# The first pair's rows picked by matmuls of zeros and ones, the first four pairs cut by half of the queries, and one more drain on GpSimd

## The chip, the core and the metric

One core of a Trainium2 chip runs the whole program. The core has five engines, each with a queue of its own that it works off in order: TensorE (PE, with its weight loads shown as PEld), VectorE (DVE), ScalarE (ACT), GpSimd (POOL) and SyncE (SP, which here only issues transfers). Transfers are issued from the queues of SP, ACT and POOL and are carried out by 16 DMA engines. The metric is the device time of one execution in microseconds (us), less being better.

## The reference

Four batches of 1,024 rows of 256 numbers go through an attention layer with 16 heads of 16 numbers, a layer norm, a mixture of eight experts of which each row takes two, and a second layer norm. The change lies in the attention; its core, cut to what matters:

```python
q = einsum('bsc,oc->bso', x, wq)            # k and v likewise, then split in 16 heads of D = 16
q_mag, k_mag = softplus(q), softplus(k)
q_embed = stack([q_mag * cos(qp), q_mag * sin(qp)])   # 32 numbers for each head and row
k_embed = stack([k_mag * cos(kp), k_mag * sin(kp)])   # kp is qp and a bias of the head
attn = softmax(einsum('bhsd,bhtd->bhst', q_embed, k_embed) / sqrt(D))
x = layernorm(x + (attn @ v) @ wo)
x = layernorm(x + experts(x))               # top 2 of 8, each with room for 640 rows
```

## The kernel before

**Work.** A batch has 16 heads, taken as 8 pairs, four in each of two groups f of 8 heads. A pair's scores are 2 heads x 1,024 queries x 1,024 keys. They are made twice. First, row by row of queries (`score_half`, L684, the matmul on L693), only to take the maxima: each 128x512 block is reduced on VectorE (L697). Then, with keys on the partitions, in `key_scores` (matmul L725), the maxima are subtracted by a small matmul of ones with two rows (L740), ScalarE takes the exponential (L747), and TensorE multiplies with the values (L761). Before that second pass, `max_parts` (L699 on) splits the 2 heads x 2 halves of maxima into two numbers each and `max_rows` transposes them (L716) and copies them (L718).

**Steps.** The loop on L971 walks 256 steps: a pair has eight, one for each 128 keys. A step holds four matmuls of each of the kinds L693 (for the next pair's maxima), L725 and L740, two exponentials of 128x1024 and eight matmuls of L761, plus what the table `todo` hangs on it: embeddings of later heads, transposes of x, values, stores.

**Embeddings.** `embedding` (L353) makes 8 heads' worth of q or k for 512 rows: a matmul (L370), softplus on ScalarE (L387 to L389), its last sum on VectorE or GpSimd (L391 or L393), the product with a table of cos and sin (L399), and a split in a rounded part and a rest (L404/L406 and L408), since the score matmuls read tiles of the type `F32R`. It leaves them with (position in the head, head) on the partitions. A pair needs another order: 32 numbers of one head below each other, parts repeated. The kernel gets this by storing the embedding in DRAM (L416) and loading the rows that a pair wants (`load_qk`, L421, transfers on L435 and L439), for every pair, the first too.

**The start.** Before the loop (L902 to L963) x is transposed (L322), the four embeddings of group 0 (k and q, two halves of 512 rows each) are made in their fast form (all of it on ScalarE and VectorE), stored and loaded again; q's on GpSimd's queue, k's on SP's. Then come all 32 maxima of pair 0 with, beside them, the values (L339) and one embedding of group 1, both halves of its q; `second_key_table` makes group 1's table of angles on ScalarE and GpSimd. Only then `max_parts(0)`, `max_rows(0)` and step 0. Step 0 also holds eight score matmuls of pair 1.

**The order** is written by hand (`tc.manual_schedule`): each engine takes its instructions in the order of the program text.

**The end.** Each expert's output rows are sent by indirect transfers from GpSimd's queue (`sent`, L1193; L1170 and L1269 are the others). The last expert sends five blocks as they come from VectorE. The program ends on L1346, where every engine drains and they meet.

Of the kernel before, what the change touches and what calls it, by code (L numbers as in the profile page):

```python
# [28 lines left out]
def kernel(  # L29
# [72 lines left out]
    with ExitStack() as actx:  # L102
# [70 lines left out]

        w_in = {w: aconst.tile([P, KC, DIM], F32, name=f"w{w}_sb") for w in "qk"}
# [39 lines left out]
        def key_table(h):  # L214

            cols = halves[h]
            for i, c in enumerate((nb4, sb4)):
                nc.vector.tensor_scalar(kt0[:, i, cols], cs[:, 1 - i, cols], c[:, 0:1], None, ALU.mult)
            for i in range(2):
                nc.vector.scalar_tensor_tensor(  # L220
                    kt0[:, i, cols], cs[:, i, cols], cb4[:, 0:1], kt0[:, i, cols],
                    ALU.mult, ALU.add,
                )

        def second_key_table(h):

            cols = halves[h]
            a = p4.tile([P, 2, HS], F32, tag="pt", name=f"kta_{h}")
            kt = p4.tile([P, 2, HS], F32, tag="pt", name=f"kt_{h}")
            for i, c in enumerate((nb4, sb4)):  # L230
                nc.scalar.activation(a[:, i, :], cs[:, 1 - i, cols], AF.Copy, scale=c[:, 1:2])
                nc.scalar.activation(kt[:, i, :], cs[:, i, cols], AF.Copy, scale=cb4[:, 1:2])
            for i in range(2):
                nc.gpsimd.tensor_tensor(kt[:, i, :], kt[:, i, :], a[:, i, :], ALU.add)
            store_table(2, h, kt)
# [117 lines left out]
        def embedding(b, f, w, h, fast=False, tab=None, pauses=()):  # L353
# [14 lines left out]
            ps = bank(f"ep_{name}", fast)  # L368
# [32 lines left out]
            parts = p2.tile([P, 2, 2, HS], F32R, tag="parts", name=f"parts_{name}")  # L401
            for i in range(2):
                if fast:
                    nc.scalar.copy(parts[:, 0, i, :], e[:, i, :])  # L404
                else:
                    nc.gpsimd.tensor_copy(parts[:, 0, i, :], e[:, i, :])  # L406
            for i in range(2):
                fine.tensor_tensor(  # L408
                    parts[:, 1, i, :], e[:, i, :], parts[:, 0, i, :], ALU.subtract
                )  # L410
            yield
            to = embed[b, f, w]
            by = nc.gpsimd if fast and w == "q" else nc.sync
            for p in range(2):
                for i in range(2):
                    by.dma_start(  # L416
                        to[2 * p + i, :, :, cols].rearrange("d m s -> (d m) s"),
                        parts.bitcast(F32)[:, p, i, :],
                    )

        def load_qk(u, cols=slice(0, S), what="qk", by=nc.sync):  # L421


            b, p = divmod(u, NU)
            f, p = divmod(p, NU // NF)
            if u not in qks:
                qks[u] = big.tile([P, 4, S], F32R, tag="big", name=f"qk_{u}")
            raw = qks[u].bitcast(F32)
            for h in range(2):
                q, k = (  # L430
                    embed[b, f, w][:, :, 2 * p + h, cols].rearrange("k d s -> (k d) s") for w in "qk"
                )
                for i in range(4 if "q" in what else 0):
                    lo = 32 * (i // 2)
                    by.dma_start(  # L435
                        raw[32 * i : 32 * (i + 1), 2 * h, cols], q[lo : lo + 32, :]
                    )
                for i in range(2 if "k" in what else 0):
                    by.dma_start(raw[64 * i : 64 * (i + 1), 2 * h + 1, cols], k)  # L439
# [244 lines left out]
        def score_half(u, k, j):  # L684


            i, s = divmod(k, 4)
            if u not in nms:
                nms[u] = small.tile([P, 4, 4, 2], F32, tag="nm", name=f"nm_{u}")
            qk, h = qks[u], s % 2  # L690
            lo = HS * (s // 2) + P * i
            ps = bank(f"s_{u}_{k}_{j}")
# [4 lines left out]
            nc.vector.tensor_reduce(nms[u][:, i, s, j : j + 1], ps, AX.X, ALU.max, negate=True)  # L697

        def max_parts(u):  # L699

            nm = nms.pop(u)
            m = m_sb[u % 2].rearrange("p i (s c) -> p i s c", c=32)
            both = small.tile([P, 4, 4, 2], F32, tag="nm_parts", name=f"nm_parts_{u}")
            nc.vector.tensor_reduce(both[:, :, :, 0], nm, AX.X, ALU.min)
# [7 lines left out]
        def max_rows(u, rotate=False):  # L712

            ps = bank(f"mp_{u}", rotate)
            for i in range(4):
                nc.tensor.transpose(ps[:, i * P : (i + 1) * P], m_sb[u % 2][:, i, :], ident)  # L716
            mts[u] = p2.tile([P, 512], F32R, tag="mt", name=f"mt_{u}")
            nc.scalar.copy(mts[u], ps)  # L718

        def key_scores(u, c, h):  # L720

            qk = qks[u]
            ps = ps_st.tile([P, 2, HS], F32, tag="st", name=f"st_{u}_{c}_{h}")
            for f in range(2):
                nc.tensor.matmul(  # L725
                    ps[:, f, :],
                    qk[:, 2 * h + 1, c * P : (c + 1) * P],
                    qk[:, 2 * h, f * HS : (f + 1) * HS],
# [5 lines left out]
        def exponentials(u, c, tiles):  # L734

            for f in range(2):
                for h in range(2):
                    s = 2 * f + h
                    rows = slice(32 * s, 32 * s + 2)
                    nc.tensor.matmul(  # L740
                        tiles[h][:, f, :], ones_r[rows, :], mts[u][rows, :],
                        start=False, stop=True,
                    )
            pts[u, c] = []
            for h in range(2):
                pt = p4.tile([P, 2, HS], F32, tag="pt", name=f"pt_{u}_{c}_{h}")
                nc.scalar.activation(pt, tiles[h], AF.Exp)  # L747
                pts[u, c].append(pt)

        def weighted_values(u, c):  # L750

            if c == 0:
                avs[u] = ps_1.tile([P, 512], F32, tag="av", name=f"av_{u}")
            av, pt = avs[u], pts.pop((u, c))
            p = u % NU
            f, p = divmod(p, NU // NF)
            for n in range(2):
                cols = slice(n * DIM, (n + 1) * DIM)
                for s in range(4):
                    h = s % 2  # L760
                    nc.tensor.matmul(  # L761
                        av[32 * s : 32 * (s + 1), cols],
                        va[f][:, c, 2 * p + h, :],
                        pt[h][:, s // 2, cols],
                        start=(c == 0 and n == 0),
                        stop=(c == NT - 1 and n == 1),
                    )
            if c == NT - 1:
                av_sb = p2.tile([P, 512], F32, tag="avs", name=f"avs_{u}")
                nc.scalar.copy(av_sb, av)  # L770
                avs[u] = av_sb
                if by_rows(u):
                    collect(u)

        def by_rows(u):
            return u < B * NU - NU // NF

        def collect(u):

            b, p = divmod(u, NU)  # L780
            f, p = divmod(p, NU // NF)
            if p == 0:
                nums[b, f] = p2.tile([P, 2, HS], F32, tag="num", name=f"num_{b}_{f}")
                sums[b, f] = dram.tile([2, FH, HS], F32, name=f"sums_{b}_{f}")
            av_sb = avs.pop(u)
            for n in range(2):
                for h in range(2):
# [562 lines left out]
```

## Time and profile before

| what | us |
|---|---|
| time, median of 3 runs (1432.48 to 1434.82) | 1434.66 |
| the profiled execution | 1435.0 |
| its span, first to last instruction | 1433.2 |
| TensorE busy | 1360.3 (95%) |
| VectorE busy | 888.3 (62%) |
| ScalarE busy | 732.8 (51%) |
| GpSimd busy | 410.5 (29%) |
| maxima on VectorE, L697, 1,024 of 684 ns | 646.3 |
| exponentials, L747, 512 of 1021 ns | 496.2 |

The page cuts the span in 40 slices of 35.8 us and gives each engine's busy share in each as a digit in tenths; PEclk is the share of its full clock that TensorE was granted. The answers of the trace by stretches of time give the same in microseconds, with the count of instructions in brackets; the timeline lists instructions by start and duration, equal neighbours merged, with the idle time before them and what ended it. TensorE's ends are modelled, so that neighbouring durations overlap; start to start is the surer reading.

### The profile page before, as it was taken

What the parts mean: (1) busy time and instruction counts of PE and PEld (TensorE: products, weight loads), DVE (VectorE), ACT (ScalarE), POOL (GpSimd) and SP (SyncE); (2) the same over time, 40 slices, a digit from 0 to 9 for tenths busy, and PEclk for the clock granted to TensorE, in tenths of its full rate; (3) what the DMA queues carried; (4) which work ended last, traced back from release to release, by engine and by line L of the source; (5) the groups of instructions that cost most, each with busy time, mean ns of one, the idle gap of its engine ahead of it and who ended that gap; (6) DMA issues with size and microseconds to landing.
All of it is one profiled execution on the core that took longest, in us unless ns stands there. A gap on an engine that the chain in (4) does not pass through costs nothing. (4 is left out here: it accounts for less than half of the span.)

```text
span 1433.2 us, 24396 instructions
## 1 busy us (share of the span) xinstructions
PE 1360.3 (95%) x9314; PEld 856.8 (60%) x9314; DVE 888.3 (62%) x1930; ACT 732.8 (51%) x1000; POOL 410.5 (29%) x436
## 2 busy tenths in 40 slices
PE   5899999999999999999999999999995499999996
PEld 3455555656655565565556556555643277777775
DVE  7767766667876666787766567787724343333334
ACT  5365666565556656556675755655562122222221
POOL 5640034250001647100065530000301314444542
PEclk8899999999999999999999999999997699999998
DMA  7856367374543746454466452234210445334211
GB/s 241 257 177 189 101 170 207 87 233 107 151 122 95 225 145 181 116 165 99 129 183 190 126 169 65 64 84 118 74 64 3 138 152 183 110 122 133 77 44 40
DMA packets 107315, 191.23 MB, mean 133 GB/s; under 512 B 19633, under 2 KB 56178, under 8 KB 107072
## 3 DMA queue, kind: packets, MB, share of 16 engines
q1 hardware_dynamic: 96192, 167.80, 40.4%
q0 software_dynamic: 9888, 20.01, 4.5%
q10 hardware_dynamic: 1120, 1.87, 0.4%
q8 instruction: 73, 1.20, 0.4%
q14 instruction: 42, 0.34, 0.1%
HBM read 119.32 MB, written 73.63 MB: 135 GB/s over the span
## 5 line engine op out<-in xcount | busy, mean ns | idle before, releaser
L697 DVE TENSOR_REDUCE nm<-s 128x1 f32<-128x512 f32 x1024 | 646.3, 684 | 240.5 <-PE s L693 232.2
L747 ACT ACTIVATE pt<-st 128x1024 f32<-128x1024 f32 x512 | 496.2, 1021 | 371.1 <-PE st L740 360.3
L693 PE MATMUL s<-qk 128*128 128x512 f32 x1024 | 387.9, 438 | 13.6 <-DVE parts_q L408 8.3
L725 PE MATMUL st<-qk 128*128 128x512 f32 x1024 | 307.1, 399 | 3.2 <-ACT pt L747 3.1
L761 PE MATMUL av<-pt,va 128*32 128x256 f32 x4096 | 274.7, 385 | 0.5 <-ACT pt L747 0.5
L693 PEld LDWEIGHTS s<-qk 128*128 128x128 f32 x1024 | 179.6, 190 | 121.4 <-DVE nm L697 49.9
L725 PEld LDWEIGHTS st<-qk 128*128 128x128 f32 x1024 | 181.9, 188 | 66.4 <-ACT pt L747 33.1
L761 PEld LDWEIGHTS av<-pt,va 128*32 128x32 f32 x4096 | 107.0, 109 | 107.2 <-issue 61.8
L644 POOL DMA_INDIRECT slots_in<-held,scatter_idx x64 | 62.7, 979 | 290.0 <-DVE scatter_idx L640 211.9
L393 POOL TENSOR_TENSOR soft_q<-y_q,soft_q 128x512 f32<-128x512 f32 x14 | 17.9, 1280 | 441.6 <-ACT soft_q L389 441.6
L1251 PE MATMUL op<-w,h 128*128 128x256 f32 x640 | 144.1, 379 | 0.0
L1232 PE MATMUL hp<-slots_t,w 128*128 128x320 f32 x512 | 140.4, 435 | 0.0
L740 PE MATMUL st<-mt,ones_r 2*128 2x512 f32 x1024 | 129.3, 494 | 0.7 <-ACT mt L718 0.7
L1251 PEld LDWEIGHTS op<-w,h 128*128 128x128 f32 x640 | 119.4, 190 | 15.9
L1232 PEld LDWEIGHTS hp<-slots_t,w 128*128 128x128 f32 x512 | 98.0, 192 | 40.2 <-issue 0.4
L740 PEld LDWEIGHTS st<-mt,ones_r 2*128 2x128 f32 x1024 | 49.1, 182 | 90.3 <-issue 89.0
L1239 ACT ACTIVATE h<-hp,b_sb 128x640 f32<-128x640 f32 x64 | 50.8, 794 | 87.0 <-PE hp L1232 87.0
L1266 DVE TENSOR_TENSOR o<-op,b_sb 128x256 f32<-128x256 f32 x35 | 14.9, 425 | 91.9 <-PE op L1251 91.9
L1267 ACT ACTIVATE o<-o,w 128x256 f32<-128x256 f32 x35 | 17.8, 508 | 103.2 <-issue 72.1
L1269 POOL DMA_INDIRECT y_rank<-o,rows x35 | 35.6, 1018 | 97.9 <-ACT slots_t L1085 42.8
L1193 POOL DMA_INDIRECT out_dram<-row,rows x40 | 41.5, 1038 | 43.9 <-DVE row L1148 14.1
L399 POOL TENSOR_TENSOR e_k<-soft_k,tab_k 128x512 f32<-128x512 f32 x28 | 35.4, 1285 | 46.4 <-DMA tab_k<-table 45.9
(211 smaller groups left out, 1008.4 us busy)
## 6 DMA issues: line engine op xcount, KB each, us to landing
qk<-embed_q SPq DMA_DIRECT2D x248, 128.0 KB
qk<-embed_k SPq DMA_DIRECT2D x124, 256.0 KB
embed_k<-parts_k SPq DMA_DIRECT2D x64, 256.0 KB
w<-in_w_dram SPq DMA_DIRECT2D x16, 1024.0 KB
embed_q<-parts_q SPq DMA_DIRECT2D x56, 256.0 KB
y_rank<-zero SPq DMA_DIRECT2D x8, 1024.0 KB
tab_k<-table SPq DMA_DIRECT2D x14, 512.0 KB
tab_q<-table SPq DMA_DIRECT2D x12, 512.0 KB
```

Of the source, the lines that this page charges most:

```text
L644: nc.gpsimd.indirect_dma_start(out=scatter_views[2 * t + k], out_offset=bass.IndirectOffsetOnAxis(ap=scatter_idx[:, k, t : t + 1], axis=0) ...
L693: nc.tensor.matmul(ps, qk[:, 2 * h, lo : lo + P], qk[:, 2 * h + 1, j * HS : (j + 1) * HS], start=True, stop=True,)
L697: nc.vector.tensor_reduce(nms[u][:, i, s, j : j + 1], ps, AX.X, ALU.max, negate=True)
L725: nc.tensor.matmul(ps[:, f, :], qk[:, 2 * h + 1, c * P : (c + 1) * P], qk[:, 2 * h, f * HS : (f + 1) * HS], start=True, stop=False,)
L740: nc.tensor.matmul(tiles[h][:, f, :], ones_r[rows, :], mts[u][rows, :], start=False, stop=True,)
L747: nc.scalar.activation(pt, tiles[h], AF.Exp)
L761: nc.tensor.matmul(av[32 * s : 32 * (s + 1), cols], va[f][:, c, 2 * p + h, :], pt[h][:, s // 2, cols], start=(c == 0 and n == 0), stop=(c ...
L1193: nc.gpsimd.indirect_dma_start(out=out_views[t], out_offset=bass.IndirectOffsetOnAxis(ap=to[:, 0, t : t + 1], axis=0), in_=row[:, t, :], i ...
L1232: nc.tensor.matmul(ps[:, i, 0:half], w1_sb[:, k, c * P : (c + 1) * P], s_t[:, k, i * half : (i + 1) * half], start=(k == 0), stop=(k == KC ...
L1239: nc.scalar.activation(h_t[:, c, :].rearrange("p (i n) -> p i n", i=2), ps[:, :, 0:half], AF.Gelu, bias=b1_sb[:, e, c : c + 1],)
L1251: nc.tensor.matmul(ps, h_t[:, c, t * P : (t + 1) * P], w2_sb[:, c, :], start=(c == 0), stop=(c == HC - 1),)
L1269: nc.gpsimd.indirect_dma_start(out=y_views[e * ST + t], out_offset=bass.IndirectOffsetOnAxis(ap=to[:, 1, t : t + 1], axis=0), in_=o_sb, in ...
```

## The change

1. **Rows by matmuls.** Pair 0 no longer goes through DRAM. On GpSimd two masks `picks` of zeros and ones are built (two fills, four selections, two copies), and `move_first` multiplies them with the embeddings' parts in SBUF: 32 matmuls of 128x512 in 8 accumulations, each copied by ScalarE to the tile from which the scores read. The parts are still stored for later pairs, all on SP's queue now, so that GpSimd's queue loses 8 stores and 16 loads and SP's loses 8 loads and gains 8 stores.
2. **Halves.** The first four pairs (group 0 of batch 0) become two units each, one for each half of 512 queries, of four steps with 256 keys each. The loop still has 256 steps. A unit needs only 16 maxima before its first step. `max_parts`, `max_rows` and the collection of results come once for each unit, so twice for these pairs.
3. **Other steps.** The last embedding of group 0 (q, second half) takes the slow form on GpSimd. The second half's angles for k are worked out between the other pieces of VectorE's queue, the third and fourth copy of x go to ScalarE. Group 1's q embeddings, values and table move from the start into the loop (embeddings at steps 4, 6, 8 and 10; values at steps 2 and 13; table at steps 0 to 3). Pair 1's load is issued after four stores of tables instead of before them; pair 2's at step 4 instead of 0.
4. **The maxima ahead** of the loop are dealt out by a small planner: each unit's must be done two steps before it starts, as evenly as that allows.
5. **A drain** on GpSimd's queue in the last expert, behind the five transfers that send the expert before it.

```diff
+        picks = p1.tile([P, 2, 2, 13, HD], F32R, tag="os", name="picks")
+        for h in range(2):
+            pick = p2.tile([P, 2, 13, HD], F32, tag="y", name=f"pick_{h}")
+            nc.gpsimd.memset(pick, 0.0)
+            for w, (first, apart) in enumerate(((5, 2), (3, 4))):
+                blocks = pick[:, w, first : first + apart + 1 : apart, :]
+                nc.gpsimd.affine_select(
+                    out=blocks, in_=blocks, compare_op=ALU.not_equal, fill=1.0, base=-h,
+                    pattern=[[0, 2], [-FH, HD]], channel_multiplier=1,
+                )
+            nc.gpsimd.tensor_copy(picks[:, h], pick)
...
-            by = nc.gpsimd if fast and w == "q" else nc.sync
...
+        def move_first(w, cols, parts):
+            if 0 not in qks:
+                qks[0] = big.tile([P, 4, S], F32R, tag="big", name="qk_0")
+            k = w == "k"
+            for h in range(2):
+                ps = bank(f"rows_{w}_{h}_{cols.start}", True)
+                for p in range(2):
+                    for c in range(2):
+                        at = c + (2 if k else 4) * p
+                        first = (3 if k else 5) - at
+                        nc.tensor.matmul(
+                            ps,
+                            picks[:, h, int(k), first : first + 8, :].rearrange("p b d -> p (b d)"),
+                            parts[p][:, c, :],
+                            start=(p == 0 and c == 0),
+                            stop=(p == 1 and c == 1),
+                        )
+                yield
+                nc.scalar.copy(qks[0][:, 2 * h + k, cols], ps)
+                yield
...
+        for i in range(B * NU):
+            for h in range(2) if i < NU // NF else (None,):
+                starts.append(starts[-1] + lasting[-1] if units else 0)
+                units.append((i, *divmod(i // (NU // NF), NF), i % (NU // NF), h))
+                lasting.append(NT if h is None else NT // 2)
...
+        for n in range(NS):
+            n_items = max([-((given - i) // (d - n + 1)) for d, i in due if d >= n], default=0)
+            most = max(i for first, i in may if first <= n)
+            ahead[n] = items[given : min(given + n_items, most)]
+            given += len(ahead[n])
...
+            mk0, mq0 = moving("k", 0), moving("q", 0)
+            for work in (mk0, mq0, mk0, mq0, q1):
                 run(work)
-            load_qk(0, halves[0], "k")
...
+            for i in range(2):
+                score_half(0, 2 * i, 0, True)
+            for work in (k1, q1, q1):
...
+            mq1 = moving("q", 1)
+            for _ in range(4):
+                run(mq1)
+            for _ in max_parts(0):
+                pass
+            max_rows(0, rotate=True)
+            run(q1)
             for h in range(2):
                 store_table(0, h, cs[:, :, halves[h]])
                 store_table(1, h, kt0[:, :, halves[h]])
+            once("k", 1)
+            once("q", 1)
+            load_qk(1)
             late_constants()
-            works = [embedding(0, 1, "q", h, tab=cs, pauses=(0, 1)) for h in range(2)]
...
-                if n == 0:
-                    for k in range(4):
-                        for j in range(2):
-                            score_half(1, k, j)
...
+                if e == E - 1:
+                    nc.gpsimd.drain()
```

## The prediction

> **What bounds the kernel.** I read the page's slices first, then stretches of 5 us over the start, the timelines of the engines there, and last what GpSimd does at the end.
>
> ```profile
> PE   5899999999999999999999999999995499999996
> ...
> PEclk8899999999999999999999999999997699999998
> ```
>
> TensorE is busy over 90% nearly everywhere. There the kernel gains only by fewer matmuls, and this change adds some. What can be gained lies where the digit is low: slices 1 and 2, the dip near slice 30 (which the change leaves alone) and the end. The start by stretches (start:end, length; busy time and count of PE, PEld, DVE, ACT, POOL; granted clock; DMA share, GB/s):
>
> ```profile
> 15.00:20.00 5.00, 5.00 (x23) 2.98 (x22) 4.06 (x8) 4.18 (x8) 0.29 (x1) 1.00 0.31 113
> 20.00:25.00 5.00, 2.27 (x21) 2.08 (x19) 4.96 (x9) 3.71 (x7) 2.60 (x5) 1.00 0.82 304
> 25.00:30.00 5.00, 0.00 (x0) 0.00 (x0) 4.96 (x9) 3.98 (x8) 4.14 (x10) 0.56 0.71 208
> 30.00:35.00 5.00, 2.15 (x4) 1.33 (x5) 1.66 (x7) 1.88 (x4) 1.99 (x3) 0.50 1.04 393
> ...
> 60.00:65.00 5.00, 4.86 (x12) 2.43 (x12) 3.30 (x6) 2.03 (x3) 2.21 (x2) 0.50 1.03 386
> 65.00:70.00 5.00, 5.00 (x14) 2.86 (x13) 4.04 (x7) 0.00 (x0) 0.00 (x0) 0.50 0.90 229
> 70.00:75.00 5.00, 4.47 (x40) 2.16 (x40) 2.80 (x5) 1.94 (x2) 0.00 (x0) 1.00 1.02 252
> ```
>
> TensorE stands from 22.3 to 30.5: the embeddings go to DRAM and back. Its clock then falls to half, and again at 60, in the loop's first two steps. VectorE is full from 20 to 30, so without the detour it is the next limit. The timelines (start, duration) give the marks of my sum:
>
> ```profile
> 30.53 0.76 PE L693 MATMUL s<-qk 128*128 128x512 f32 x1 [8.26 <-DVE parts_q L408]
> ...
> 58.81 0.65 PE L716 MATMUL mp<-ident,m 128*128 128x128 f32 x4 [2.09 <-DVE m L710]
> ```
>
> ```profile
> 61.04 1.94 ACT L747 ACTIVATE pt<-st 128x1024 f32<-128x1024 f32 x2 [0.95 <-PE st L740]
> ```
>
> ```profile
> 170.85 1.94 ACT L747 ACTIVATE pt<-st 128x1024 f32<-128x1024 f32 x2 [1.44 <-PE st L740]
> ```
>
> The exponentials of step 0 start at 61.04 and those of step 28 at 170.85. In the order of the two built programs TensorE's last 5,704 matmuls, from the transposes at step 27 on, are the same; so what step 28 gains the whole loop gains. The end, by what stands on the program's last line (the count, then shortest, median and longest in ns):
>
> ```profile
> L1346 POOLq DRAIN  x3: 51/93/8552, 1423.9 to 1432.9; - x3
> ```
>
> ```profile
> 1424.11 0.97 POOL L1193 DMA_INDIRECT out_dram<-row,rows  x1 [2.48 <-DVE row L1148]
> ```
>
> GpSimd's last transfer is issued by 1425.08, the drain ends at 1432.42 (1423.87 + 8.55), and the span ends at 1433.2. SP has seen every landing by 1426.9, where its own drain stands. So for 5.5 us everything waits for GpSimd alone.
>
> **Part 1, the start to step 0.** Up to 14.45 the queues agree, but for two copies of x (1.27 on VectorE) that ScalarE takes (1.1). From there I lay VectorE's new order end to end with its rows' durations: sum and products of k0 0.69 + 1.29; two table pieces 1.0; q0 2.0; k0's rests 1.29; a table piece 0.7; q0's rests 1.29; a table piece 0.7; k1 2.0: this ends at 25.1. The rows of k0 can be picked when its rests are there (20.7), those of q0 at 22.5: 23.0 for the last matmul. TensorE then makes q1's embedding (1.9: 1.88 at 15.10 and at 16.82 in its timeline) to 24.9, and the first maxima reach VectorE at 25.3: two maxima, k1's rests 1.29, two maxima: 29.4. ScalarE meanwhile has q1's softplus (2.5) and two copies of rows (0.59 each) and frees the next scores at 29.6; 12 maxima from 30.2 at 0.64 (11 in 7.00 in the timeline) end at 37.9. TensorE puts half of the values (1.87: 32 records took 3.73) and q1's eight row matmuls (0.22 each) behind the last score: 40.2. A copy, the parts and the transposes follow as at 58.81, at 41.6, and step 0's exponentials at 44.4 (2.2 behind the transposes before, 2.8 now, since eight score matmuls stand between). q1 itself goes through GpSimd: 7.4 as at 44.58 to 52.0, from 28.4 to 35.8: covered by 4 us. Masks: two fills, four selections (0.37 each), two copies (0.58): about 3.2, done by 16, needed at 18. GpSimd's and SP's transfers that leave this stretch free nobody else: the gain is 61.04 - 44.4 = **16.6**.
>
> **Part 2, what is moved or added behind step 0.** A plain step takes 3.49 (exponentials at 106.59, 110.07, 113.56). Up to step 28 the changed kernel has four more `max_rows` (0.37 each, by a step with one) 1.5; both halves of values 3.7; q's two embeddings (1.89 each: a step of 5.38) 3.8; and 12 more score matmuls (0.25) 3.0, since pair 0 had 32 before step 0 and now 16, and 4 of the next unit lie before the mark. Sum **12.0** given back. The 32 row matmuls are in part 1. Units of half the queries have as many score, exponential and value instructions in all as before: nothing. Group 1's four embeddings on GpSimd, 7.4 each, start at step 4 near 60, the first behind pair 2's loads (its table by 69): done near 99, stored before step 16 near 110 loads them, and their scores come at step 23: nothing.
>
> **Part 3, stalls in the first steps.** Before, step 28 came 109.8 behind step 0. By pieces: 28 steps 97.6, three `max_rows` 1.1, two embeddings 3.8, two transposes 0.8, eight extra scores 2.0: 105.3. So 4.5 were lost, at half clock and behind ten maxima. The changed kernel has 16 maxima for three steps, 10.2 on VectorE against some 11.4 on TensorE: close, I charge 1.5. ScalarE gets two activations more a step (1.4), 3.4 of 3.8: 0.5. Pair 1's rows are first needed as step 3 begins: 44.4 and three steps 10.5, scores 1.0, values 1.9, less the 2.4 of a step ahead of its exponentials and less the 1.0 of a product with values that step 0 has not: 54.4. SP's queue: q1's stores to 37 behind GpSimd, four tables 4.1, twelve loads 7.2: last issued at 48.7 (the tile waits for two copies of weights on VectorE at 41). At 250 GB/s, the rate of 40 to 50, tables and loads (2.1 MB each) land at 51 to 54. I charge 0.5. Later loads (pair 2's issued near 65, needed past 85) have room, though 24 more small stores of results and ten loads of constants stand in SP's queue. Stalls **2.5**, from 0.5 to 8.
>
> Start: 16.6 - 12.0 + 4.5 - 2.5 = **6.6**.
>
> **Part 4, the drain.** It stands behind the five sends of the last expert but one, free at 1406.16; behind it in the queue are only the five last sends, the first due at 1410.29. No row shows a drain with few transfers behind it. Below: nothing comes back. Above: the wait of 5.5 goes wholly. The Trainium skill ("VectorE: DVE Perf Modes", section "The DRAIN you can't avoid") tells of drains from the preamble and postamble of about 12 ns on all engines. By that the added drain costs and returns nothing, and the sum is 1428.1. The row says 8552 ns, and the two drains right behind it, with nothing outstanding, 93 and 51. I take the row: the time goes with the transfers not yet settled, 210 on GpSimd over the program and none drained since the start. Settling 181 of the new 186 earlier leaves five, and 5.4 comes back. Its own price: from 1406.2 it may take the 7.3 that the last needed from 1425.08, to 1413.5. The first two sends slip (1.28 each to issue), the third at 1417.2 is on time; only past 1419 would the last be late. GpSimd's tiles are reused by none after. So **5.4**, ends 0 and 5.5.
>
> **Sum.** Span 1433.2 - 6.6 - 5.4 = 1421.2; with the 1.8 around it 1423.0. The median of the runs is 0.3 below the profiled execution: **1422.7**.
>
> **Rivals.**
> *The drain returns nothing* (its cost is a constant of the end): 1422.7 + 5.4 = 1428.1. For it: no second example. Against it: 93 and 51 ns. Chance 0.2.
> *The start pays little*: pair 1's rows land late. Pair 2's load, issued to 70.2, had the DMA engines full until 80; if pair 1's takes the same 10 behind 48.7, it lands at 58.7, TensorE waits 4.2, and a clock fallen to half costs more. The start is worth 0 to 2 and the time 1427 to 1430. For it: the DMA share near 1 whenever tables and rows move. Against it: no embeddings are stored beside it. Chance 0.12.
> *Slower: the clock.* From 17.3 to 22.5 TensorE has only eight row matmuls, 1.7 us of work. A stretch with 1.00 of 3.41 busy (56.37 to 59.78) was followed by half clock, one with 2.75 was not. If it falls near 22 and stays, the 14.8 of matmuls between 22.5 and step 0 (24 for rows and 16 scores at 0.22, q1's embedding 1.9, values 3.7, transposes 0.4) take twice as long, step 0 comes 10 late, and the loop's start loses 5 more: 1422.7 + 15 = 1437.7. It decides once half clock covers 12 us of work at full clock, that is 24 us of time. The skill ("TensorE: Matmul & The Clock Gate", section "What's actually happening") lets one busy window of about 3.4 us lift it, which would price a cold start at 1.7; here TensorE was busy from 60 to 70.02 at half, which prices it at 5.1. I take the row, but scores waiting for maxima made that stretch thin, and q1's embedding is dense. Chance 0.06.
> *Both parts as summed*, 0.62, its own range 1418 to 1426.
>
> **Numbers.** The range takes in the bounds of the stalls and a drain without return: 1417.5 to 1429.5. What can be told from no change is 0.2%, 2.9 us: faster below 1431.8 0.92, same 0.04, slower 0.04 (the clock, less the cases in which it recovers).
>
> **What would show it.** Rows picked: no gap of 8 us before the first score, first maximum near 25, step 0's exponentials near 44, step 28's near 164. Part 3: TensorE's idle before pair 1's first score under 1 us, clock 1.00 from 40 on. The drain: one of several us on GpSimd in the last expert, and the last one shorter than 4. Wrong would be exponentials of step 0 past 50, half clock in steps 0 to 2, or a last drain still of 8 us.

## The result, and the profile after

The changed kernel takes 1424.74 us (median of 6 runs, 1423.33 to 1425.70), the kernel before 1434.74 in the runs beside it (6 runs, 1432.26 to 1435.73): a ratio of 0.9934, with a 95% interval of 0.9921 to 0.9946. The forecast was 1422.7, from 1417.5 to 1429.5. The span of the profiled execution goes from 1433.2 to 1423.3.

I read the profile after in the order of the prediction. First the page's slices (busy tenths of TensorE, and its granted clock):

```profile
PE   7999999999999999999999999999996399999998
...
PEclk9999999999999999999999999999998599999999
```

The first two clock digits, 8 and 8 before, are 9 and 9. The dip near slice 30 is still there. Then the same stretches of the start (busy time and count by engine, clock, DMA share, GB/s):

```profile
15.00:20.00 5.00, 4.01 (x10) 1.53 (x8) 3.94 (x7) 3.79 (x7) 1.41 (x8) 1.00 0.03 11
20.00:25.00 5.00, 3.76 (x8) 2.14 (x8) 5.00 (x9) 3.86 (x7) 0.00 (x0) 0.70 0.86 319
25.00:30.00 5.00, 4.82 (x17) 2.96 (x16) 4.27 (x8) 4.30 (x8) 0.47 (x1) 0.96 0.60 222
30.00:35.00 5.00, 4.90 (x26) 3.53 (x25) 4.54 (x9) 1.76 (x3) 4.92 (x6) 1.00 0.27 100
...
60.00:65.00 5.00, 4.88 (x33) 2.67 (x32) 3.61 (x6) 4.10 (x7) 1.28 (x1) 1.00 0.17 64
65.00:70.00 5.00, 5.00 (x35) 2.94 (x34) 2.96 (x5) 4.05 (x7) 1.28 (x1) 1.00 1.03 241
70.00:75.00 5.00, 5.00 (x33) 2.44 (x32) 3.48 (x7) 2.49 (x5) 0.00 (x0) 1.00 1.02 229
```

Between 20 and 35 TensorE now works 13.5 of 15 us, where it worked 4.4. Its clock is at half only from 22.00 to 25.41 and full from then on. The marks, from TensorE's and ScalarE's timelines:

```profile
26.24 1.50 PE L755 MATMUL s<-qk 128*128 128x512 f32 x4
...
42.20 0.66 PE L783 MATMUL mp<-ident,m 128*128 128x128 f32 x4 [1.12 <-DVE m L777]
```

```profile
45.18 1.94 ACT L816 ACTIVATE pt<-st 128x1024 f32<-128x1024 f32 x2 [1.70 <-PE st L809]
...
165.60 1.94 ACT L816 ACTIVATE pt<-st 128x1024 f32<-128x1024 f32 x2 [1.95 <-PE st L809]
```

The first score has no wait for memory. Step 0's exponentials come at 45.18 (61.04 before), step 28's at 165.60 (170.85 before): the start is worth 5.25. At the end, the drains by their lines (the added one on L1339, the program's last on L1459; count, then shortest, median and longest in ns) and GpSimd's timeline:

```profile
L1339 POOLq DRAIN  x1: 9088/9088/9088, 1398.0 to 1398.0; - x1
```

```profile
L1459 POOLq DRAIN  x3: 51/97/2885, 1419.6 to 1423.1; - x3
```

```profile
1400.55 0.97 POOL L1303 DMA_INDIRECT out_dram<-row,rows  x1 [0.30 <-issue]
1408.11 0.97 POOL L1303 DMA_INDIRECT out_dram<-row,rows  x1 [6.59 <-DVE var_e L1240]
...
1419.80 0.97 POOL L1303 DMA_INDIRECT out_dram<-row,rows  x1 [2.48 <-DVE row L1258]
```

A drain's record starts while the sends ahead of it are still being issued, so I count from the end of the last issue. The added drain ends at 1407.07, 5.55 behind the end of the issue at 1400.55, and the next send follows 1.0 later; the timeline puts that wait down to VectorE, but the send was queued behind the drain. The last drain is 2.89 long, 8.55 before. From the end of the last send to the end of the span it is 8.14 before and 2.57 after.

Splitting the span at the last exponentials of attention (1080.58 before, 1075.89 after) gives the account: the part up to there is 4.69 shorter and the part behind it 5.20 (352.64 to 347.44): 9.9 in all.

### The profile page after: what moved, and what is told of

Same layout as the page of the kernel before. It is cut to its first block, busy times and chain, and to the rows that moved or that the text cites. A ratio compares the mean times of both kernels' runs of the same rounds, so it can differ in the third digit from the quotient of the medians.

```text
span 1423.3 us, 24542 instructions
## 1 busy us (share of the span) xinstructions
PE 1365.4 (96%) x9362; PEld 863.9 (61%) x9362; DVE 885.8 (62%) x1931; ACT 740.8 (52%) x1025; POOL 408.3 (29%) x427
## 5 line engine op out<-in xcount | busy, mean ns | idle before, releaser
L755 PE MATMUL s<-qk 128*128 128x512 f32 x1024 | 383.4, 434 | 3.6 <-DVE nm L759 2.2
L795 PE MATMUL st<-qk 128*128 128x512 f32 x1024 | 303.8, 398 | 2.6 <-ACT pt L816 2.6
L1364 PEld LDWEIGHTS op<-w,h 128*128 128x128 f32 x640 | 119.5, 190 | 15.9
```

The source lines that it names most:

```text
L755: nc.tensor.matmul(ps, qk[:, 2 * h, lo : lo + P], qk[:, 2 * h + 1, j * HS : (j + 1) * HS], start=True, stop=True,)
L795: nc.tensor.matmul(ps[:, x, :], qk[:, 2 * h + 1, k * P : (k + 1) * P], qk[:, 2 * h, q * HS : (q + 1) * HS], start=True, stop=False,)
L1364: nc.tensor.matmul(ps, h_t[:, c, t * P : (t + 1) * P], w2_sb[:, c, :], start=(c == 0), stop=(c == HC - 1),)
```

## The experiments

My theory: the start gains because TensorE no longer stands still while the first pair's rows go through memory, less the work pushed behind step 0; the end gains because the added drain settles most of GpSimd's transfers under other work. The rivals: the start's gain is the clock, or comes from the halves alone; the end's gain comes from fewer transfers on GpSimd; a drain is a fixed price.

The experiments ran on other chips of the kind, where the kernel before took 1443 to 1447 us and where nearly all kernels have one or two waits of about 2 us in the loop (near 505 and 770 us) that the first chip's traces lack. Each ratio is to the kernel before on the same chip, and single profiles differ by many us in the middle of the loop: from the fifth pair to the last exponentials it is 901.8 in the changed kernel on the first chip and 907.0 in the same kernel on another. So I compare marks in the start and behind the last exponentials. "Fifth pair" is the start of the VectorE instruction that splits that pair's maxima; "rest" is from the last exponentials to the end of the span.

| kernel | first score | step 0's exponentials | fifth pair | rest | ratio, 95% interval |
|---|---|---|---|---|---|
| before (first chip) | 30.53 | 61.04 | 179.16 | 352.6 | 1 |
| changed (first chip) | 26.24 | 45.18 | 174.08 | 347.4 | 0.9934 [0.9921, 0.9946] |
| e1_no_drain | 27.82 | 46.84 | 175.68 | 351.0 | 0.9942 [0.9922, 0.9962] |
| e2_before_drain | 32.12 | 61.93 | 179.80 | 346.8 | 0.9961 [0.9946, 0.9977] |
| e3_rows_by_dram | 34.11 | 59.44 | 189.74 | 347.1 | 1.0012 [0.9999, 1.0024] |
| e4_whole_pairs | 25.82 | 56.49 | 177.11 | 347.5 | 0.9965 [0.9951, 0.9979] |
| r_after (the changed kernel again) | 25.50 | 44.56 | 173.47 | 347.1 | 0.9925 [0.9912, 0.9938] |
| e5_drain_every_expert | 26.06 | 45.37 | 174.18 | 346.5 | 0.9947 [0.9934, 0.9959] |
| e6_rows_first | 25.95 | 44.87 | 173.62 | 347.3 | 0.9940 [0.9926, 0.9954] |
| e7_rows_first_den_later | 25.79 | 44.71 | 173.59 | 346.8 | 0.9920 [0.9907, 0.9933] |
| e9_drain_0_1_last | 26.33 | 45.27 | 174.16 | 347.5 | not comparable |
| e10_before_warm | 42.35 | 75.71 | 192.06 | 353.0 | 1.0097 [1.0078, 1.0116] |
| e11_parts_between | 25.65 | 44.03 | 172.91 | 347.1 | 0.9906 [0.9889, 0.9923] |
| e12_warm_second | 30.65 | 63.22 | 180.82 | 352.6 | 0.9992 [0.9979, 1.0006] |

The first four experiments ran on one chip, and e2 has the old start; so e2 is the measure for their starts. r_after to e7 ran on another, e9 to e11 on a third, e12 on a fourth. The start of e1 is 2 us late for a reason that lies ahead of the edits (shown at the whole pairs).

**The changed kernel without the drain.**

```diff
-                if e == E - 1:
-                    nc.gpsimd.drain()
```

> The changed kernel without the drain in the last expert. Theory (the drain lets GpSimd settle its transfers beside the last expert's matmuls): the last drain is long again, 7 to 8.5 us, and the time is 1424.7 + 5.6 = 1430.3, from 1429 to 1431.5. Rival (the end became shorter for another reason, such as 24 transfers less on GpSimd's queue): the last drain stays under 4 us and the time within 1 us of 1424.7.

The drain on the last line:

```profile
L1456 POOLq DRAIN  x3: 51/97/7165, 1432.2 to 1439.9; - x3
```

It is 7.17 long, and the part behind the last exponentials is 351.0: 3.9 more than r_after has with the drain, and 1.7 less than before. So with 24 fewer transfers on GpSimd (210 to 186) the end is 1.7 shorter with no drain added; 1.4 of that is the last drain itself (8.55 to 7.17). The rival of fewer transfers has that part and no more. The ratio came out lower than expected (1429 to 1431.5 would be 0.996 to 0.998); its interval just reaches the nearer end. In the times the drain of the changed kernel is not shown: 0.9942 without it, 0.9934 and 0.9925 with it, and the intervals overlap. It is shown by the traces: the part behind the last exponentials is 351.0 to 353.0 in the four kernels without the drain and 346.5 to 347.5 in the ten with it.

**The kernel before with the drain.** The same two lines in the last expert of the kernel before.

> The kernel before with only the drain added at the same place. Theory: 1434.7 - 5.5 = 1429.2, from 1428 to 1430.5; the drain in the middle takes 9 to 10 us for some 205 transfers, the last one about 2.9, and the five last sends end at the same moment as before. Rival: 1434.7.

The two drains, added and last:

```profile
L1228 POOLq DRAIN  x1: 10480/10480/10480, 1413.6 to 1413.6; - x1
```

```profile
L1348 POOLq DRAIN  x3: 51/92/2891, 1435.2 to 1438.7; - x3
```

As expected. The rest goes from 352.6 to 346.8, which is 5.8, with a ratio of 0.9961. The drain works alone, and by the same size. Its own cost is nil: from the end of the last issue ahead of it to the end of the last send it is 19.2 us here and 19.2 without a drain in e1.

**Rows through memory, all else as changed.** No masks, no row matmuls; the first pair's rows are stored and loaded in the new order, q's loads on GpSimd.

```diff
-            mk0, mq0 = moving("k", 0), moving("q", 0)
-            for work in (mk0, mq0, mk0, mq0, q1):
-                run(work)
+            run(k0)
+            by_dram("k", halves[0], nc.sync)
+            run(q0)
+            by_dram("q", halves[0], nc.gpsimd)
+            run(q1)
```

> The changed kernel, but pair 0's rows are stored and loaded through DRAM again (k on SP's queue, q's loads on GpSimd's, no masks, no row matmuls); halves, order of steps and drain stay. Theory (the detour was what the start waited for): the first score comes at 33 to 36 instead of 26, step 0's exponentials at 51 to 56 instead of 45.2, and of that the time keeps 6 to 10: 1431 to 1435. Rival (VectorE's chain of embeddings is the limit anyway and hides the detour): within 2 us of 1424.7.

TensorE's timeline:

```profile
34.11 3.59 PE L732 MATMUL s<-qk 128*128 128x512 f32 x7 [14.88 <-DMA qk<-embed_q]
...
44.52 2.04 PE L732 MATMUL s<-qk 128*128 128x512 f32 x4 [4.14 <-DMA qk<-embed_k]
```

The first score is where I expected it; step 0's exponentials are 3.4 past my range. TensorE waits 14.88 and then 4.14 for rows, and its clock is at half from 22 to 49 and again from 56 to 63. Step 0 comes only 2.5 before that of e2, but the work pushed behind it stays: at the fifth pair this start is 9.9 behind e2's and 15.7 to 16.3 behind the changed kernel's (first chip and r_after). The halves without the row matmuls are a loss; the ratio is near 1 only because the drain pays 5.5 back.

**Whole pairs, all else as changed.**

```diff
-            for h in range(2) if i < NU // NF else (None,):
+            for h in (None,):
...
+            for j in range(2):
+                for i in range(4):
+                    for h in range(2):
+                        score_half(0, 4 * i + 2 + h, j, True)
             for _ in max_parts(0):
                 pass
```

> The changed kernel without halves: pair 0's 32 maxima all stand before step 0, every pair is one unit of eight steps; rows by matmuls and the drain stay, and pair 1's load is issued before the second 16 maxima. Theory of the prediction's part 2 (most of what the halves win is given back, since the other 16 scores and four more sets of maxima's transposes come later on TensorE): step 0's exponentials 8 to 10 us later, near 54, the time only 2 to 4 above 1424.7. Rival (the maxima on VectorE lie wholly on the path, 10.2 us): 1433 to 1435.

VectorE's timeline:

```profile
40.95 0.69 DVE L759 TENSOR_REDUCE nm<-s 128x1 f32<-128x512 f32 x1 [2.28 <-PE s L755]
41.87 9.06 DVE L759 TENSOR_REDUCE nm<-s 128x1 f32<-128x512 f32 x15 [0.23 <-PE s L755]
```

The other 16 maxima cost 9.75 us of VectorE ahead of step 0, where TensorE has little else: it waits 3.28 ahead of the transposed maxima. e1 can't be the measure as it stands, since its weights landed late, ahead of all that the edits touch. VectorE's first copy of them in e1, and then here:

```profile
10.26 0.42 DVE L193 COPY wk_sb<-twice 128x128 f32<-128x128 f32 x2 [3.26 <-DMA twice<-in_wk_dram]
```

```profile
8.68 0.42 DVE L193 COPY wk_sb<-twice 128x128 f32<-128x128 f32 x2 [1.84 <-DMA twice<-in_wk_dram]
```

So I count from the first score. Step 0's exponentials come 30.7 behind it here and 19.0 in e1: 11.7 later, more than the 8 to 10 that I expected. The fifth pair comes 151.3 behind it here and 147.3 to 148.1 in the eight kernels with halves and row matmuls, 147.9 in e1. So of the 11.7 only 3.4 is kept: the other work has to be done in any case. Against the old start (179.16 and, in e2, 179.80) the fifth pair at 177.11 is 2.0 to 2.7 earlier. So the rows by matmuls with whole pairs are worth 2.0 to 2.7, and the halves on top 3.4; together that is about the 5.1 to 5.7 by which the changed kernel's fifth pair is ahead of the first chip's old one (174.08 and, in r_after, 173.47). The ratio, 0.9965, is higher than expected, and its interval overlaps the expected 0.995 to 0.996.

**The changed kernel once more.**

> The changed kernel itself, once more, as the measure for the others on this chip. If the first measurement holds, the ratio to the kernel before lies in 0.992 to 0.995 and the first pair's fifth group of maxima comes 4 to 5 us earlier than in a profile of the kernel before. If the runs on the second chip (both edits alone together worth 14 us, where the change is worth 10) mean that the two parts take from each other, the ratio here is under 0.992 as well only by chance; if they were noise, the trace's own parts stay at 4 to 5 us for the start and 5.5 us for the end.

The ratio is 0.9925, and the marks up to the fifth pair are within 0.8 us of the first chip's. By the ratios the two edits alone (e1 and e2) sum to some 14 us, where both together take 10 to 11 off; the intervals are wide enough for that, and the marks in the start and at the end show no such excess.

**A drain in every expert but the first.**

```diff
-                if e == E - 1:
+                if e >= 1:
```

> The changed kernel with a drain of GpSimd in every expert but the first, where it had one in the last expert. If a drain's length goes with the transfers issued on GpSimd since the drain before (19 to 27 ns for each, on top of some 1.7 us of landing), the drain of the second expert, behind some 90 transfers, ends 3.5 to 4 us behind the end of the issue before it, the later ones, behind 14 or 15 each, about 2 us; the last expert's is no longer 5.5. If a drain's length is a price of its own, all of them end about 5.5 us behind the issue before them. The time stays within 2 us of the changed kernel by either, since GpSimd has that slack in every expert.

The drains, and GpSimd's timeline around the first of them:

```profile
L1338 POOLq DRAIN  x7: 5105/5670/11260, 1200.6 to 1407.5; - x7
```

```profile
1203.37 0.97 POOL L1303 DMA_INDIRECT out_dram<-row,rows  x1 [0.30 <-issue]
1212.79 0.97 POOL L1381 DMA_INDIRECT y_rank<-o,rows  x1 [8.45 <-issue]
```

The first drain, with 91 transfers behind it, ends at 1211.85, 7.51 behind the last issue; the six others, with 15 each, 1.79 to 2.46. The last expert's is at 2.09, where the changed kernel's, the first of its program, is at 5.55. So a drain has no fixed price: 15 transfers since the drain before cost less than 91. But the size was wrong: 91 cost more than the 181 of the changed kernel. The time is 3.0 us above r_after's, more than the 2 expected, and the runs of the two don't overlap. But the programs differ only behind the last exponentials, and that part is 346.5 against 347.1: the seven drains cost nothing there. The profiles differ ahead of it (1086.4 against 1080.4 at the last exponentials), where both programs are the same; why is not shown.

**Three drains.**

```diff
-                if e == E - 1:
+                if e in (0, 1, E - 1):
                     nc.gpsimd.drain()
...
-                    if e == E - 1:
+                    if e in (0, 1, E - 1):
```

> The changed kernel with three drains: in the first, the second and the last expert. In the kernel with a drain in every expert but the first, the drain of the second expert, behind 91 transfers, ended 7.5 us behind the end of the last issue, the others, behind 15, 1.8 to 2.5. If what counts is the transfers since the drain before, the one of the first expert, behind some 76, ends 6 to 7.5 us behind its last issue, the second expert's, behind 15, about 2, and the last one's, behind 90, about 7. If the second expert's place made it long (its transfers among the heavier loads there), it stays near 7 with 15 behind it. If a transfer's price sinks once the queue has wrapped, the last one ends 4 us or less behind its issue.

The edit changed more than the drains: by its second part the first two experts end as the last one does, each block normalized and sent at once, so the output is wrong. The time is not compared; GpSimd's transfers are as many as in e5, and only the drains are read. The first expert's drain ran at 15.6 us already, behind 12 transfers, so it says little. The second expert's has 79 behind it and ends 6.51 behind the last issue; the last one's has 90 and ends 7.40 behind. So it isn't the place: 90 cost in the last expert what 91 cost in the second. Why 181 and 186 cost only 5.55 and 5.96, and 205 and 210 only 6.94 and 7.35, stays open; with so many, part may have been settled on the way.

**Maxima ahead of the last rows.** `max_parts(0)` and `max_rows(0)` stand ahead of the four pieces of `mq1` instead of behind them.

> The changed kernel with the row maxima of the first unit put ahead of the row matmuls of the second query half, so that their copies no longer stand ahead of the negation on ScalarE. VectorE's wait of 3.25 us for the negated parts goes to under 1 us, TensorE's idle 1.1 us ahead of the first transposed maxima goes, and step 0's exponentials come 1 to 2.5 us earlier. If the work behind step 0 is TensorE's bound, the later rows cost the same and 0 to 1.1 us are kept at the fifth unit's maxima; if the first q rows of the second half are wanted at once, nothing is kept. In the time within 1.5 us of the changed kernel.

The same places on VectorE and on TensorE:

```profile
39.80 0.19 DVE L777 TENSOR_REDUCE m<-nm_parts 128x16 f32<-128x32 f32 x1 [1.40 <-ACT nm_parts L773]
```

```profile
40.05 0.66 PE L783 MATMUL mp<-ident,m 128*128 128x128 f32 x4 [1.12 <-DVE m L777]
```

VectorE's wait falls from 3.25 only to 1.40, and TensorE still stands 1.12 us, for now nothing lies between the last values and the transposes. Nothing is kept. The order of the copies on ScalarE made VectorE's wait longer, but TensorE's idle time did not hang on it.

**Reciprocals one step later.**

```diff
-            for c in (1, 2, 5, 6):
+            for c in (1, 3, 5, 6):
```

> The one before, and the reciprocals of the denominators one step later in the batches behind the first (step 3 in place of step 2), so that their transfer has some 4 us more. If the waits for that transfer are what took about 1 us of the start's gain back, the waits of 1 to 3 us at the three reciprocals go, and the PE gaps of 0.7 to 1.7 us just behind them; 1 to 3 us less than the changed kernel. If other work comes late in their place, the gaps stay and the time is the same.

VectorE's timeline near 326, in e6 and then here:

```profile
326.42 0.55 DVE L884 RECIPROCAL den<-den 128x64 f32<-128x64 f32 x1 [2.22 <-DMA den<-sums]
```

```profile
327.43 0.54 DVE L884 RECIPROCAL den<-den 128x64 f32<-128x64 f32 x1
```

All three waits are gone, and the stretch around the first, from one pair's maxima to the next pair's, is 0.92 shorter than in e6 (31.44 to 30.52). In the time, 0.9920 against 0.9940 with intervals that overlap.

**Parts between the rows.**

```diff
-            for c in (1, 2, 5, 6):
+            for c in (1, 3, 5, 6):
...
-            for _ in range(4):
-                run(mq1)
+            run(mq1)
             for _ in max_parts(0):
                 pass
+            for _ in range(2):
+                run(mq1)
             max_rows(0, rotate=True)
+            run(mq1)
```

> The changed kernel with the maxima's parts put between the two halves of the row matmuls of the second query half, so that TensorE has a row matmul to do while VectorE and ScalarE make the parts, and neither waits for the other; the reciprocals of the denominators one step later, as in the kernel before it. TensorE's 1.1 us ahead of the first transposed maxima goes under 0.3, step 0's exponentials come 0.8 to 1.3 us earlier against the first score, and the fifth unit's maxima as much. If something else is late there (the second half's q rows for the next scores), the idle time shows ahead of those scores and under 0.4 us is kept. In the time 0 to 2.5 us less than the changed kernel, a ratio to before of 0.9915 to 0.993.

TensorE's timeline:

```profile
40.39 0.60 PE L783 MATMUL mp<-ident,m 128*128 128x128 f32 x4
40.74 0.47 PE L755 MATMUL s<-qk 128*128 128x512 f32 x1
41.66 0.50 PE L755 MATMUL s<-qk 128*128 128x512 f32 x1 [0.45 <-ACT mt L785]
```

The 1.12 is gone, and 0.45 comes back two instructions later. From the first score to step 0's exponentials it takes 18.4 (19.1 in r_after), and the fifth pair keeps the 0.7: between the two expectations. With 0.9906 it has the lowest ratio, with the reciprocals of e7 (0.9920) in it, but the interval overlaps the changed kernel's (0.9912 to 0.9938): that it is faster as a whole isn't shown.

**Unread matmuls in the old start.** The kernel before, with matmuls on x whose results nobody reads.

```diff
+            warm("a", 19)
             n = 0
...
+                        if n in (0, 25, 27, 29, 31):
+                            warm(n, 5 if n == 0 else 1)
...
+            warm("b", 4)
             max_rows(0, rotate=True)
+            warm("c", 1)
```

> The kernel before, with 28 matmuls of 128x128 on 512 columns more, whose results nobody reads, in the two places where TensorE stood idle and the granted clock then fell to a half: 19 ahead of the first score, 5 behind it, 4 between the scores of the first pair's end, 4 and 1 around the transposed maxima. They lie in waits, so they cost under 1 us themselves. If the half clock is what made the old start long, the clock stays near 1.00 from 20 to 75 us, step 0's exponentials come 2 to 4 us earlier than the 61 to 62 us of before, step 28's 5 to 8 us earlier, and the ratio is 0.9945 to 0.9975. If the waits themselves (rows through memory, maxima one by one on VectorE) made it long, the clock rises and the time of the first pairs stays within 1.5 us, ratio 0.999 to 1.001.

Stretches of the start:

```profile
35.00:40.00 5.00, 5.00 (x13) 2.28 (x12) 0.00 (x0) 0.00 (x0) 1.80 (x4) 1.00 0.86 300
...
65.00:70.00 5.00, 5.00 (x16) 2.78 (x15) 4.46 (x8) 0.72 (x2) 4.09 (x4) 1.00 0.72 276
```

I had mis-sized it: each of these matmuls ran as two passes of 0.43, and the first waited to 26.3 for VectorE, so the first score came 12 us late and the ratio says nothing. But the clock stayed full to 80, and that tells something. VectorE's first maxima in the kernel before, and then here:

```profile
38.13 1.29 DVE L697 TENSOR_REDUCE nm<-s 128x1 f32<-128x512 f32 x2 [1.40 <-PE s L693]
40.10 1.98 DVE L697 TENSOR_REDUCE nm<-s 128x1 f32<-128x512 f32 x3 [0.68 <-PE s L693]
```

```profile
47.72 1.89 DVE L697 TENSOR_REDUCE nm<-s 128x1 f32<-128x512 f32 x3 [3.84 <-PE s L693]
49.86 3.40 DVE L697 TENSOR_REDUCE nm<-s 128x1 f32<-128x512 f32 x5 [0.26 <-PE s L693]
```

From the second maximum to the ninth it took 6.6 us before, most of it at half clock, and 4.9 here; from the ninth to the 26th, at full clock in both, 12.3 and 12.1. So the half clock cost the old start about 1.7 us: TensorE had an embedding beside these scores and no wait from 34.04 to 40.29, and VectorE waited for it. (The 22.5 us in the expectation below runs to the end of the unread matmul behind the last score. From the second score to the last it is 21.4 here and 22.2 before.) From step 0 to the fifth pair it took 116.4, before 118.1.

**Only the second place.** Four of them between the last scores and two ahead of the transposed maxima.

> The kernel before with unread matmuls at the second of the two places only: 4 of them one by one between the last scores of the first pair and 2 ahead of the transposed maxima (in the run with 28 of them, each took two passes of 0.43 us, so these are 5.1 us, of which the scores' waits for VectorE and the 2.1 us ahead of the transposed maxima hide nearly all). That run, with the clock at 1.00 throughout, did the first pair's scores in the same time as before, 22.5 us for the last 31, and step 0 to the fifth pair's maxima in 116.4 where before took 118.1. If that difference is the clock's, the stretch from 59.8 to 70 us stays at 1.00 here, step 0's exponentials stay within 0.6 us of before against the first score, the next step's come 8.3 to 8.8 us behind them (before 10.1), and the fifth pair's maxima 116.2 to 116.8 behind. If it came of the late start alone (rows already landed), 118 as before. In the time at most 2 us less than before, ratio 0.998 to 1.000.

The stretch that was at half before:

```profile
65.00:70.00 5.00, 4.61 (x10) 2.66 (x11) 4.65 (x8) 0.16 (x1) 0.00 (x0) 0.71 0.95 243
```

The clock is at half for 3.41 us (67.08 to 70.49) instead of 10.24. Step 0's exponentials come 2.1 later against the first score, since the matmuls were not hidden as I expected, and the fifth pair 117.6 behind them, 0.5 less than before and 0.3 less than in e2. So in the loop's first steps the half clock was worth 0.3 to 1.7 us, the larger figure from e10, whose loop also began 14 us later. That it is little fits step 0's scores, in the kernel before at half clock and here, at full clock up to 67.08:

```profile
60.87 5.96 PE L693 MATMUL s<-qk 128*128 128x512 f32 x10
```

```profile
64.33 4.38 PE L693 MATMUL s<-qk 128*128 128x512 f32 x7 [0.32 <-DVE nm L697]
```

Both go at about 0.60 from one to the next, which is what a maximum takes on VectorE. With the 1.7 of the first pair, my estimate for the half clock in the old start is 2.0 to 3.4 us. The changed kernel has half clock for one window of 3.41 us where the old start has it for seven (25.65 to 39.30 and 59.78 to 70.02). So the rival holds in part: some of the start's gain came by way of the clock, which fell behind two windows of 3.41 us in which TensorE was busy for 0.04 and 1.00 (from 22.23 and 56.37); no run here separates the two. Warming the old start by more matmuls gains nothing (0.9992), since step 0 comes 2.1 later for them.

## Why the prediction was right

The sign, the two mechanisms and, within its range, the sum held: 1424.74 against 1422.7. Of the 2.0 that are missing, 1.9 are in the start and the loop (4.69 shorter up to the last exponentials, where 6.6 was forecast). The terms:

- **Start to step 0**, predicted 16.6: measured 15.86. The chain on VectorE was right in kind. The first score came at 26.24, and the first maximum at 27.07 instead of 25.3. Most of that is VectorE's chain: it began at 14.88 instead of 14.45, and the sum of q0 waited for ScalarE, where the prediction had laid VectorE's pieces end to end:

```profile
18.70 0.69 DVE L412 SCALAR_TENSOR_TENSOR soft_q<-ep_q,soft_q 128x512 f32<-128x512 f32 x1 [0.99 <-ACT soft_q L410]
```

  So q0's rests were done at 23.79, not 22.5. The other 0.5 fits the clock, at half from 22.00 to 25.41, which I had only as a rival. r_after has it the other way round: no such wait and the rests done at 22.23, but all of q1's embedding at half clock and the first maximum at 26.43. From the first maximum to the end of the sixteenth it took 11.4, where I had 12.6, so part of the good fit at the transposes, 42.20 (41.6), is luck. (The pieces that I listed for VectorE add up to 25.4, not 25.1.)
- **Behind step 0**, predicted 10.0 given back (12.0 - 4.5 + 2.5): measured 10.6 (step 28 comes 120.4 behind step 0, where it was 109.8). So the start gave 5.25, not 6.6. The traces don't split this 0.6 further. I had put the 4.5 lost in the old first steps down to half clock and ten maxima; by e10, which is at full clock there and takes 108.0 for them, at most 1.8 of it was the clock's. Without the row matmuls (e3) the same given-back work made the start a loss of 9.9, and with whole pairs (e4) 2.0 to 2.7 remained, with 3.4 more from the halves: the halves pay only together with the picked rows.
- **Loop**, predicted unchanged behind step 28: 0.56 of the start's gain is lost again by the last exponentials. This is a term that the sum did not have, though 0.56 is less than the loop of one kernel differs between two chips (901.8 and 907.0 from the fifth pair on). VectorE's timeline near 326, and TensorE's behind it:

```profile
326.46 0.55 DVE L884 RECIPROCAL den<-den 128x64 f32<-128x64 f32 x1 [1.93 <-DMA den<-sums]
```

```profile
327.61 0.51 PE L755 MATMUL s<-qk 128*128 128x512 f32 x1 [0.69 <-DVE nm L759]
```

  The denominators' transfer ends while VectorE waits for it at the head of its queue, 1.93 us here and 0.87 before. That is 1.06 more, and from the pair ahead of it to the pair behind it the lead over the kernel before falls from 5.1 to 4.1. Near 588 it happens again (2.13, before 1.50; lead 3.6), near 849 the other way round (0.92, before 1.97), and the lead is 4.7. So what the wait grows by, the lead loses. e7 takes a wait of 2.22 away and 0.92 of the stretch with it, so part of a wait is covered. The same order of work is thus not the same time: a transfer may land a microsecond later.
- **Drain**, predicted 5.4: measured 5.2 behind the last exponentials. That the row (8552) and not the boilerplate drain of the Trainium skill ("VectorE: DVE Perf Modes", section "The DRAIN you can't avoid") gave the price was right: five transfers behind the last drain cost 2.89, and with 210 it was 8.55. But not all of it is the drain's: e1 shows 1.7 from the 24 transfers that left GpSimd, and 3.9 for the drain itself. I had given all to the drain, and the sum was the same since the last drain is left with five in either case. Its own price was nil as predicted, ending at 1407.1 where I allowed 1413.5.
- **Rivals.** Pair 1's rows came in time: its first score at 55.62 has no wait on TensorE. The clock did fall near 22, but one window of 3.41 us lifted it, as the Trainium skill says ("TensorE: Matmul & The Clock Gate", section "What's actually happening") and as I doubted from the 10.24 us of before. In that old stretch TensorE was busy by the records and still had three windows at half; here one sufficed. What differs in the activity of those windows is not shown by the records.

## What to carry to other kernels

A reordering that brings the first step forward is worth the idle time that it removes, not the time by which that step comes earlier: count all that was pushed behind it (here 15.9 earlier, 5.25 kept; with the rows still late, 2.5 earlier and 9.9 lost). A drain on GpSimd put where GpSimd has slack takes the settling of its transfers off the end, provided few are issued behind it. And before warming TensorE's clock, look at who sets the pace beside it: step 0's scores took no longer at half clock, since VectorE's maxima set the pace, but the first pair's, with an embedding beside them on TensorE, lost about 1.7.

## What the runs showed of the hardware

- A drain on GpSimd ends 1.68 us behind the end of the last issue with 5 transfers since the drain before, 1.8 to 2.5 with 15, 6.51 with 79, 7.40 with 90 and 7.51 with 91; but 5.55 with 181, 5.96 with 186, 6.28 with 197, 6.94 with 205 and 7.35 with 210. It rises, then steps back somewhere between 91 and 181, and rises again.
- A drain written in the first expert's text ran at 15.6 us, over a millisecond ahead of the second expert's at 1204 (e9); what moved it is not recorded. Where order matters, look up in the trace where it ran.
- A 128x512 matmul on x, of type F32, took two passes of 0.43 us at full clock (e10), where a 128x512 score from a tile of type `F32R` takes one of about 0.23: the same shape at nearly four times the price.
